# A two-layer masked attention stack in float32: from blocks of 256 tokens to two passes over blocks of 512 with seven-product projections

## The chip, the core and the metric

The kernel runs on one core of a Trainium2 chip. A core has a matrix engine (TensorE, PE in the rows; its weight loads are PEld), three engines for elementwise work (VectorE or DVE, ScalarE or ACT, GpSimd or POOL), a queue that issues transfers (SP), and on-chip memory in 128 partitions; matmul results land in PSUM, which has 8 banks. The engines run their own instruction streams in order and wait for each other by semaphores. The metric is the device time of one launch in microseconds (us). One profiled execution gives the rows that are read here.

## What is computed

The input is 128 batches of 64 tokens with 768 features, with one 64x64 adjacency matrix per batch. The tokens are normalised and clipped at zero; two layers follow, and the input is added to the result. Weights are 768x768 per layer and kind, all in float32.

```python
for l in range(L):
    m_left = jnp.einsum('bsh,oh->bso', h, W_left[l])
    m_right = jnp.einsum('bsh,oh->bso', h, W_right[l])
    u_left = jnp.einsum('bih,bjh->bij', h, m_left) / temper
    u_right = jnp.einsum('bih,bjh->bij', h, m_right) / temper
    u = u_left * adj_tri + u_left * diag_mask + u_right * jnp.swapaxes(adj_tri, 1, 2)
    delta_exp_u = jnp.exp(u) * adj
    attention = delta_exp_u / (jnp.sum(delta_exp_u, axis=2, keepdims=True) + 1e-10)
    h_lin = jnp.einsum('bsh,oh->bso', h, W_lin[l]) + b_lin[l]
    ctx = jnp.matmul(attention, h_lin)
    h = jax.nn.relu(_layer_norm(ctx, ln_a[l], ln_b[l]))
return h
```

## The kernel before

The 8192 tokens are cut into 32 blocks of 256. A unit is one block in one layer, so there are 64 units, and two neighbouring blocks alternate: both do layer 0, then both do layer 1. All six weight matrices stay on the chip. A unit runs through these parts:

- `projections` (L186): m_left and m_right, features on partitions. For each kind 6 output chunks of 6 matmuls over 256 tokens, 36 in all; two chunks share a PSUM bank, which ACT copies out (L188). Two banks take turns.
- `transposed` (L165): the *next* unit's normalised rows are turned so that features lie on partitions, 12 transposes; ACT clips them (L168 in layer 0, L171 in layer 1) into `ht`.
- `scores` (L199): 24 matmuls of 128 columns, then DVE masks (L204), ACT exponentiates (L208), DVE masks again.
- `linear` (L232): h_lin with tokens on partitions, 12 matmuls of 384 columns for each half of the block; DVE adds the bias while it empties the bank (L234). Between the halves stands `attention`: one matmul gives the row sums (L216), DVE takes the reciprocal (L221) and divides.
- `context` (L243): 4 matmuls of 384 columns; DVE takes mean and variance (L139, L140), ACT the root (L251), DVE normalises (L256). In layer 1 POOL then multiplies and adds two rows (L263, L264), DVE adds the input (L265), and POOL's queue stores the result (L267).

One matmul of the program is two instructions on PE in the trace, since the operands are float32; a transpose is one. Nothing schedules the work: every engine runs its instructions in the order in which the code emits them. `input_norm` of a coming block (L139, L149, L151, L153) is emitted at the start of a unit, ahead of that unit's projections, and behind the output work of the unit before. So ACT has the root L149 ahead of the copies L188 of the same unit, and L149 needs the statistics that DVE takes after L265, which needs POOL's L264.

## Time and profile before

| | us |
|---|---|
| median of 3 runs | 3959.29 (3958.76 to 3961.19) |
| span of the profiled execution | 3958.0 |
| PE busy | 3684.1 |
| DVE busy | 846.5 |
| ACT busy | 564.6 |
| POOL busy | 298.4 |

The profiled execution is one launch; its span runs from its first to its last instruction. Busy time is a union of instructions; PE's ends are modelled, so a price per matmul is better read from the distance of two starts than from a busy time. A number in square brackets at the end of a row is how long the engine sat idle before it, and what released it.

### The profile page before, as it was taken

The page shows a single profiled execution, that of the slowest core. Times are in us where ns is not written, and L with a number is a line of the kernel's source. Part 1 is how long each engine was busy: PE and PEld are TensorE (multiplying, and loading weights), DVE is VectorE, ACT ScalarE, POOL GpSimd, SP SyncE. Part 2 cuts the span into 40 slices and gives each one's busy share as a digit, 9 for nine tenths or more (in the row PEclk, how much of TensorE's full clock was granted, in tenths as well). Part 3 has the DMA queues.
Part 4 walks back from the last instruction along what each step waited for, and adds up shares of the span by engine and source line. Part 5 has one row for each costly group of instructions (what it writes and reads, how often), then busy time and mean ns, then how long its engine had stood idle before and what let it go on. Part 6 is the DMA issues. An engine that isn't in the chain of part 4 may idle for free.

```text
span 3958.0 us, 37169 instructions
## 1 busy us (share of the span) xinstructions
PE 3684.1 (93%) x16768; PEld 2914.2 (74%) x16768; DVE 846.5 (21%) x1826; ACT 564.6 (14%) x961; POOL 298.4 (8%) x270
## 2 busy tenths in 40 slices
PE   8989999899998999989999999999999999999997
PEld 6777777777776777777777777777777777777776
DVE  1122122221222222222222122121121211212212
ACT  1111111111111111111111111111111111111111
POOL 0010000100001000010000100000000000100001
PEclk9999999999999999999999999999999999999999
DMA  5010000100001000000000100000000000000000
GB/s 187 1 35 1 18 18 1 35 1 18 18 1 35 1 18 18 5 31 0 18 18 5 31 0 18 18 12 24 0 18 18 18 18 0 18 18 18 9 0 16
DMA packets 38942, 72.64 MB, mean 18 GB/s; under 512 B 3968, under 2 KB 25984, under 8 KB 38784
## 3 DMA queue, kind: packets, MB, share of 16 engines
q1 hardware_dynamic: 33664, 45.10, 3.9%
q0 software_dynamic: 5120, 25.17, 1.6%
q8 instruction: 131, 2.15, 0.2%
q14 instruction: 27, 0.22, 0.0%
HBM read 45.09 MB, written 25.17 MB: 18 GB/s over the span
## 4 chain that ended last, share of the span: by engine, by line
PE 83%; POOL 6%; DVE 4%; ACT 3%; issue 3%; SPq 1%; DMA 0%; POOLq 0%
PE mm L186 44%; PE mm L232 25%; PE aux L199 9%; PE cx L243 4%; POOL z L263 3%; POOL z L264 3%; DVE st L139 2%; ACT ht L171 1%; DVE z L265 1%; ACT mt L188 1%; PE aux L165 1%; POOL out_dram L267 0%; SPq L74 0%; ACT ht L168 0%; DVE mv L140 0%
## 5 line engine op out<-in xcount | busy, mean ns | idle before, releaser
L186 PE MATMUL mm<-ht,w_l 128*128 128x256 f32 x4608 | 1075.7, 396 | 202.4 <-ACT mt L188 202.4
L186 PEld LDWEIGHTS mm<-ht,w_l 128*128 128x128 f32 x4608 | 917.6, 200 | 363.4 <-ACT mt L188 214.9
L232 PE MATMUL mm<-w_n,ht 128*128 128x384 f32 x3072 | 1012.0, 486 | 0.0
L186 PE MATMUL mm<-ht,w_r 128*128 128x256 f32 x4608 | 1005.0, 379 | 0.0
L186 PEld LDWEIGHTS mm<-ht,w_r 128*128 128x128 f32 x4608 | 875.6, 190 | 118.9
L232 PEld LDWEIGHTS mm<-w_n,ht 128*128 128x128 f32 x3072 | 574.0, 190 | 373.0
L204 DVE TENSOR_TENSOR um<-aux,wm 64x256 f32<-64x256 f32 x128 | 54.0, 422 | 2053.0 <-PE aux L199 2052.2
L188 ACT COPY mt<-mm 128x512 f32<-128x512 f32 x384 | 221.0, 584 | 1517.3 <-PE mm L186 1517.3
L263 POOL TENSOR_TENSOR z<-z,a_row 128x768 f32<-128x768 f32 x64 | 116.1, 1813 | 3537.3 <-issue 3271.4
L199 PE MATMUL aux<-ht,mt 128*128 128x128 f32 x3072 | 359.8, 277 | 8.1 <-ACT ht L171 8.1
L199 PEld LDWEIGHTS aux<-ht,mt 128*128 128x128 f32 x3072 | 347.9, 192 | 18.0 <-ACT ht L171 15.7
L234 DVE TENSOR_TENSOR hl<-mm,blin 128x384 f32<-128x384 f32 x256 | 142.8, 558 | 662.8 <-PE mm L232 662.8
L243 PE MATMUL cx<-hl,att 128*128 128x384 f32 x512 | 175.6, 486 | 0.0
L251 ACT ACTIVATE sd<-var 128x2 f32<-128x2 f32 x64 | 13.0, 203 | 1084.7 <-DVE var L249 1084.7
L165 PE MATMUL aux<-ident,z 128*128 128x128 f32 x768 | 109.8, 280 | 42.7 <-ACT ht L171 23.1
L243 PEld LDWEIGHTS cx<-hl,att 128*128 128x128 f32 x512 | 97.3, 190 | 67.8
L139 DVE BATCH_NORM_STATS2 st<-cx 128x6 f32<-128x384 f32 x256 | 131.8, 557 | 48.0 <-PE cx L243 46.9
L165 PEld LDWEIGHTS aux<-ident,z 128*128 128x128 f32 x768 | 87.7, 142 | 64.5 <-ACT ht L171 30.7
L256 DVE TENSOR_SCALAR z<-cx,mv,rs 128x768 f32<-128x768 f32 x128 | 132.0, 1073 | 2.3
L264 POOL TENSOR_TENSOR z<-z,b_row 128x768 f32<-128x768 f32 x64 | 115.3, 1802 | 5.0
L265 DVE SCALAR_TENSOR_TENSOR z<-z,x 128x768 f32<-128x768 f32 x64 | 61.3, 958 | 240.2 <-POOL z L264 240.2
L171 ACT ACTIVATE ht<-aux,b_col,a_col 128x256 f32<-128x256 f32 x192 | 91.1, 577 | 0.0
(35 smaller groups left out, 700.5 us busy)
## 6 DMA issues: line engine op xcount, KB each, us to landing
x<-in_x_dram SPq DMA_DIRECT2D x32, 768.0 KB, 4.9
out_dram<-z POOLq DMA_DIRECT2D x64, 384.0 KB, 2.6
w_l<-in_w_left_dram SPq DMA_DIRECT2D x6, 768.0 KB, 7.6
w_r<-in_w_right_dram SPq DMA_DIRECT2D x6, 768.0 KB, 10.6
w_n<-in_w_lin_dram SPq DMA_DIRECT2D x6, 768.0 KB, 10.7
adj<-in_adj_dram SPq DMA_DIRECT2D x32, 128.0 KB, 5.7
blin<-in_b_lin_dram SPq DMA_DIRECT2D x2, 384.0 KB, 9.2
a_row<-in_ln_a_dram SPq DMA_DIRECT2D x1, 384.0 KB, 8.4
```

The lines of the kernel that those rows point to most:

```text
L139: nc.vector.bn_stats(st[:, n, :], src[:, n, :])
L165: nc.tensor.transpose(p[:, c, q * P:(q + 1) * P], z[:, q, (c0 + c) * P:(c0 + c + 1) * P], ident)
L171: nc.scalar.activation(ht[:, c0 + c, :], p[:, c, :], AF.Relu, bias=b_col[:, c0 + c:c0 + c + 1], scale=a_col[:, c0 + c:c0 + c + 1])
L186: nc.tensor.matmul(p[:, o, :], w[:, c, (o0 + o) * P:(o0 + o + 1) * P], ht[:, c, :], start=(c == 0), stop=(c == C - 1))
L188: nc.scalar.copy(mt[:, k, o0:o0 + 2, :], p)
L199: nc.tensor.matmul(p[:, q, k, :], mt[:, k, c, t], ht[:, c, t], start=(c == 0), stop=(c == C - 1))
L232: nc.tensor.matmul(p, ht[:, c, q * P:(q + 1) * P], W[l, "n"][:, c, cols], start=(c == 0), stop=(c == C - 1))
L234: nc.vector.tensor_add(hl[:, q, cols], p, blin[l][:, cols])
L243: nc.tensor.matmul(p[:, n, :HH], att[:, q, :], hl[:, q, n * HH:(n + 1) * HH], start=True, stop=True)
L256: nc.vector.tensor_scalar(z[:, q, :].rearrange("p (n d) -> p n d", n=2), ps[q][:, :, :HH], mv[:, q, 0:1], rs[:, q:q + 1], op0=ALU.subtract ...
L263: nc.gpsimd.tensor_mul(z[:, q, :], z[:, q, :], a_row)
L264: nc.gpsimd.tensor_add(z[:, q, :], z[:, q, :], b_row)
```

## The change

Each layer is now two passes over all tokens, in 16 blocks of 512. `pass_one` computes the projections, the scores and the attention, and stores the attention (and in layer 0 the clipped, turned input) in DRAM. `pass_two` loads the features and the attention again, computes h_lin, the context and the normalisation, and stores the next layer's features in DRAM, or the output. In the code of the order below, X, Y, Z and V are PSUM tiles of a bank each, `n` is a buffer that holds m, h_lin or the features to be stored, `ts` holds sums of token blocks.

The three projections are no longer multiplied out in full but by seven products of half matrices: the weight is cut into four blocks A11 to A22 of 384x384, the features of a block into B11 to B22 (384 features by 256 tokens each). Four sums of weight blocks (S1 to S4, on DVE or POOL, once per weight) and four sums of token blocks (T1 to T4, on POOL, once per block and pass) go into the seven products. For 512 tokens, m_left or m_right takes 63 matmuls of 256 columns where it took 72, and h_lin 42 of 384 columns where it took 48. Four PSUM banks hold the products, two of them accumulate a second product in the bank of a first that has been read in between, and DVE and ACT combine them. The elementwise work of neighbouring blocks is put in a queue of closures, and `pump` emits one (pass one) or three (pass two) of them behind each product. In pass two ACT applies the normalisation (L399), where DVE did (L256). The reciprocal, the bias and the output work stay on their engines; the output is stored through SP.

All of the old body goes. The core of what comes:

```diff
+    Q = 4
+    T = Q * P
+    TH = T // 2
...
+    big = ctx.enter_context(tc.tile_pool(name="big", bufs=2))
...
+    ps_st = ctx.enter_context(tc.tile_pool(name="ps_st", bufs=1, space=bass.MemoryType.PSUM))
+    ps_aux = ctx.enter_context(tc.tile_pool(name="ps_aux", bufs=4, space=bass.MemoryType.PSUM))
...
+    queue = deque()
+    def pump(n):
+        for _ in range(min(n, len(queue))):
+            queue.popleft()()
...
+    def load_w(l, kind):
+        v = SRC[kind][l].rearrange("(c p) o -> p c o", p=P)
+        t = {}
+        for s in ("A11", "A21", "A22", "A12", "S1", "S2", "S4"):
+            t[s] = wpool.tile([P, CH, HH], F32, name=f"w_{kind}_{s}")
+        for s in ("A11", "A21", "A22", "A12"):
+            i, o = int(s[2]) - 1, int(s[1]) - 1
+            nc.sync.dma_start(t[s], v[:, i * CH:(i + 1) * CH, o * HH:(o + 1) * HH])
+        W[l, kind] = t
+    def sums_w(l, kind, eng):
+        t = W[l, kind]
+        eng.tensor_add(t["S1"], t["A21"], t["A22"])
+        eng.tensor_sub(t["S2"], t["S1"], t["A11"])
+        eng.tensor_sub(t["A21"], t["A11"], t["A21"])
+        t["S3"] = t.pop("A21")
+        eng.tensor_sub(t["S4"], t["A12"], t["S2"])
+    ORDER = (("X", "A11", "B11"), ("Y", "S2", "T2"), ("Z", "S1", "T1"), ("V", "S3", "T3"),
+             ("X", "A12", "B21"), ("Z", "S4", "B22"), ("V", "A22", "T4"))
...
+        ts = big.tile([P, 4, CH, TH], F32, name="ts")
+        TS[key] = ts
+        b = tokens_of(key)
+        queue.append(lambda: nc.gpsimd.tensor_sub(b["T1"], b["B12"], b["B11"]))
+        queue.append(lambda: nc.gpsimd.tensor_sub(b["T2"], b["B22"], b["T1"]))
+        queue.append(lambda: nc.gpsimd.tensor_sub(b["T3"], b["B22"], b["B12"]))
+        queue.append(lambda: nc.gpsimd.tensor_sub(b["T4"], b["B21"], b["T2"]))
...
+                m = M[kind]
+                bank = {}
+                for i, (at, a, t) in enumerate(ORDER):
+                    new = at not in bank
+                    if new:
+                        bank[at] = ps_st.tile([P, 512], F32, name=at)
+                    p = bank[at][:, :TH]
+                    for c in range(CH):
+                        nc.tensor.matmul(p, w[a][:, c, g * P:(g + 1) * P], b[t][:, c, :],
+                                         start=(new and c == 0), stop=(c == CH - 1),
+                                         skip_group_check=True)
+                    if i == 0:
+                        s1 = sp.tile([P, TH], F32, name="s1")
+                        nc.scalar.copy(s1, p)
+                    elif i == 1:
+                        u2 = sp.tile([P, TH], F32, name="u2")
+                        nc.vector.tensor_add(u2, p, s1)
+                    elif i == 2:
+                        u4 = sp.tile([P, TH], F32, name="u4")
+                        nc.vector.tensor_add(u4, p, u2)
+                    elif i == 3:
+                        nc.vector.tensor_add(m[:, CH + g, TH:], p, u4)
+                    elif i == 4:
+                        nc.scalar.copy(m[:, g, :TH], p)
+                    elif i == 5:
+                        nc.vector.tensor_add(m[:, g, TH:], p, u2)
+                    else:
+                        nc.vector.tensor_add(m[:, CH + g, :TH], p, u2)
+                    pump(1)
...
+            for u in range(NB):
+                if u == 0:
+                    load(0)
+                    if first:
+                        first()
+                    prepare(0)
+                    flush()
+                    load(1)
+                for g in range(CH):
+                    project(u, "l", g)
+                    if g == 0:
+                        if u:
+                            scores(u - 1, 1, "r")
+                            if u + 1 < NB:
+                                load(u + 1)
+                        if u + 1 < NB:
+                            prepare(u + 1)
+                        if u in aside:
+                            aside[u]()
+                for g in range(CH):
+                    project(u, "r", g)
+                    if g == 0:
+                        scores(u, 0, "l")
+                flush()
+            scores(NB - 1, 1, "r")
+            flush()
+    def load_h(which, l, u):
+        ht = big.tile([P, C, T], F32, name="ht")
+        nc.sync.dma_start(ht, (H0 if l == 0 else H1)[u])
+        HT[which, l, u] = ht
...
+                z = sp.tile([P, H], F32, name="z", bufs=2 if last else 4)
+                Z[u, q] = z
+                if last:
+                    xr = sp.tile([P, H], F32, name="xr", bufs=2)
+                    nc.sync.dma_start(xr, x_t[u][q])
+                def chain():
+                    mv = stat.tile([P, 2], F32, name="mv1")
+                    mean_var(mv, cx)
+                    var = stat.tile([P, 1], F32, name="var")
+                    nc.vector.tensor_scalar(var, mv[:, 1:2], UNBIASED, 1e-30, op0=ALU.mult, op1=ALU.max)
+                    yield
+                    sd = stat.tile([P, 1], F32, name="sd1")
+                    nc.scalar.activation(sd, var, AF.Sqrt)
+                    rs = stat.tile([P, 1], F32, name="rs1")
+                    nc.vector.tensor_scalar_add(rs, sd, EPS_LN)
+                    nc.vector.reciprocal(rs, rs)
+                    nb = stat.tile([P, 1], F32, name="nb1")
+                    nc.vector.scalar_tensor_tensor(nb, mv[:, 0:1], -1.0, rs, op0=ALU.mult, op1=ALU.mult)
+                    yield
+                    for n in range(2):
+                        nc.scalar.activation(z[:, n * HH:(n + 1) * HH], cx[n], AF.Identity, bias=nb, scale=rs)
+                    yield
+                    if last:
+                        nc.gpsimd.tensor_mul(z, z, rows["a"])
+                        nc.gpsimd.tensor_add(z, z, rows["b"])
+                        yield
+                        nc.vector.scalar_tensor_tensor(xr, z, 0.0, xr, op0=ALU.max, op1=ALU.add)
+                        nc.sync.dma_start(out_t[u][q], xr)
+                it = chain()
+                return [lambda: next(it, None)] * (5 if last else 4)
...
+            def finish(u, r):
+                a = context(u, r)
+                pump(1)
+                b = context(u, 2 + r)
+                for i in range(len(a)):
+                    queue.append(a[i])
+                    queue.append(b[i])
+                if not last:
+                    turn(u, r)
+            def linear(u, r, before):
+                b, w = tokens_of((2, l, u)), W[l, "n"]
+                if r == 0:
+                    HL[u] = big.tile([P, Q, H], F32, name="n")
+                hl = HL[u]
+                bank = {}
+                for i, (at, a, t) in enumerate(ORDER):
+                    new = at not in bank
+                    if new:
+                        bank[at] = ps_st.tile([P, 512], F32, name=at)
+                    p = bank[at][:, :HH]
+                    for c in range(CH):
+                        nc.tensor.matmul(p, b[t][:, c, r * P:(r + 1) * P], w[a][:, c, :],
+                                         start=(new and c == 0), stop=(c == CH - 1),
+                                         skip_group_check=True)
+                    if i == 0:
+                        s1 = sp.tile([P, HH], F32, name="s1", bufs=1)
+                        nc.vector.tensor_add(s1, p, rows["b1"])
+                    elif i == 1:
+                        u2 = sp.tile([P, HH], F32, name="u2", bufs=1)
+                        nc.vector.tensor_add(u2, p, s1)
+                        u2b = sp.tile([P, HH], F32, name="u2b", bufs=1)
+                        nc.gpsimd.tensor_add(u2b, u2, rows["b2"])
+                    elif i == 2:
+                        u4 = sp.tile([P, HH], F32, name="u4", bufs=1)
+                        nc.vector.tensor_add(u4, p, u2b)
+                    elif i == 3:
+                        nc.vector.tensor_add(hl[:, 2 + r, HH:], p, u4)
+                    elif i == 4:
+                        nc.vector.tensor_add(hl[:, r, :HH], p, rows["b1"])
+                    elif i == 5:
+                        nc.vector.tensor_add(hl[:, 2 + r, :HH], p, u2)
+                    else:
+                        nc.vector.tensor_add(hl[:, r, HH:], p, u2b)
+                    if i == 0 and before:
+                        before()
+                    pump(3)
+            for u in range(NB):
+                if u == 0:
+                    load(0)
+                    prepare(0)
+                    flush()
+                for r in range(2):
+                    before = None
+                    if u or r:
+                        before = lambda: finish(*((u, 0) if r else (u - 1, 1)))
+                    linear(u, r, before)
+                    if r == 0:
+                        if u + 1 < NB:
+                            load(u + 1)
+                        if u in aside:
+                            aside[u]()
+                    elif u + 1 < NB:
+                        prepare(u + 1)
+                        flush()
+            finish(NB - 1, 1)
+            flush()
...
+    def weights(*pairs):
+        for l, kind in pairs:
+            load_w(l, kind)
+            queue.append(lambda l=l, kind=kind: sums_w(l, kind, nc.gpsimd))
+    def start():
+        load_w(0, "l")
+        sums_w(0, "l", nc.vector)
+        load_w(0, "r")
+        sums_w(0, "r", nc.vector)
+        load_w(0, "n")
+        sums_w(0, "n", nc.gpsimd)
+    pass_one(0, start, {})
+    pass_two(0, {1: lambda: weights((1, "l")), 2: lambda: weights((1, "r"))})
+    pass_one(1, None, {1: lambda: weights((1, "n"))})
+    pass_two(1, {})```

In PE's order, a unit before stands so (one row per group of matmuls: destination, operands, columns, count; this is the second unit, with the transposes of the third):

```order
L186 MATMUL mm<-ht,w_l_85 128x256 x36
L186 MATMUL mm<-ht,w_r_89 128x256 x36
L165 MATMUL aux<-ident,z 128x128 x12
L199 MATMUL aux<-ht,mt 128x128 x24
L232 MATMUL mm<-w_n_93,ht 128x384 x12
L216 MATMUL aux<-d,bsum 128x128
L232 MATMUL mm<-w_n_93,ht 128x384 x12
L243 MATMUL cx<-hl,att_138 128x384 x4
```

PE now, from the start, one third of the left projection's outputs for 512 tokens:

```order
L204 MATMUL aux<-ident,x 128x128 x24
L235 MATMUL X<-ht,w_l_A_175 128x256 x3
L235 MATMUL Y<-ts,w_l_S_180 128x256 x3
L235 MATMUL Z<-ts,w_l_S_179 128x256 x3
L235 MATMUL V<-ts,w_l_A_176 128x256 x3
L235 MATMUL X<-ht,w_l_A_178 128x256 x3
L235 MATMUL Z<-ht,w_l_S_181 128x256 x3
L235 MATMUL V<-ts,w_l_A_177 128x256 x3
```

Where a run of 36 matmuls stood, a bank now changes after every 3, and X, Z and V are each written twice within seven products.

DVE in an output unit before, from the context's variance on (layer 1, then the coming block's statistics):

```order
L249 TENSOR_SCALAR var<-mv_801 128x2
L253 TENSOR_SCALAR rs_820<-sd_818 128x2
L254 RECIPROCAL rs_820<-rs_820 128x2
L256 TENSOR_SCALAR z<-cx,mv_801,rs_820 128x768 x2
L265 SCALAR_TENSOR_TENSOR z<-z,x 128x768 x2
L139 BN_STATS st<-x 128x6 x2
```

DVE now, in the last pass, from the second product (Y) of one `linear` to its last (V):

```order
L463 TENSOR_TENSOR u_17097<-Y,s_17056 128x384
L393 TENSOR_SCALAR rs_17103<-sd_17101 128x1
L394 RECIPROCAL rs_17103<-rs_17103 128x1
L396 SCALAR_TENSOR_TENSOR nb_17106<-mv_17079,rs_17103 128x1
L468 TENSOR_TENSOR u_17116<-Z,u2b 128x384
L405 SCALAR_TENSOR_TENSOR xr<-z,xr 128x768
L470 TENSOR_TENSOR n<-V,u_17116 128x384
L405 SCALAR_TENSOR_TENSOR xr<-z,xr 128x768
L472 TENSOR_TENSOR n<-X,b_14084 128x384
L474 TENSOR_TENSOR n<-Z,u_17097 128x384
L476 TENSOR_TENSOR n<-V,u2b 128x384
```

The two instructions that wait for POOL's output work (L265 before, L405 now) stood together after a unit's last bank was emptied; now each stands between two instructions that empty banks of the products.

POOL now, in pass two of layer 0 around the loading of a layer-1 weight (before, there are no such sums, and POOL takes no part in a projection):

```order
L465 TENSOR_TENSOR u2b<-u_6170,b_5960 128x384
L96 TENSOR_TENSOR w_l_S_6238<-w_l_A_6235,w_l_A_6236 128x1152
L97 TENSOR_TENSOR w_l_S_6239<-w_l_S_6238,w_l_A_6234 128x1152
L98 TENSOR_TENSOR w_l_A_6235<-w_l_A_6234,w_l_A_6235 128x1152
L100 TENSOR_TENSOR w_l_S_6240<-w_l_A_6237,w_l_S_6239 128x1152
L465 TENSOR_TENSOR u2b<-u_6291,b_5960 128x384
```

The four sums of a weight stand ahead of the `u2b` (L465) of the same `linear`, for which DVE's L468 waits.

## Rows read from the trace of the kernel before

**Rows 1.** The page, busy time of each engine.

```profile
PE 3684.1 (93%) x16768; PEld 2914.2 (74%) x16768; DVE 846.5 (21%) x1826; ACT 564.6 (14%) x961; POOL 298.4 (8%) x270
```

**Rows 2.** The waits: engine, line, waited for, us in total, times, longest.

```profile
PE mm L186 <- ACT mt L188: 202.4, 31, 8.4
```

**Rows 3.** The timeline around one such wait: start, length, engine, line, tiles, count.

```profile
2175.05 0.96 DVE L265 SCALAR_TENSOR_TENSOR z<-z,x 128x768 f32<-128x768 f32 x1 [4.63 <-POOL z L264]
...
2178.34 0.29 ACT L149 ACTIVATE sd<-mv,eps_in 128x2 f32<-128x2 f32 x1 [14.25 <-DVE mv L140]
2178.54 1.05 ACT L188 COPY mt<-mm 128x512 f32<-128x512 f32 x2
...
2179.16 7.62 PE L186 MATMUL mm<-ht,w_l 128*128 128x256 f32 x24 [6.46 <-ACT mt L188]
2186.62 3.62 PE L186 MATMUL mm<-ht,w_r 128*128 128x256 f32 x16
```

**Rows 4.** Stretch behind that wait: PE, PEld, DVE, ACT, POOL busy, clock, DMA, GB/s.

```profile
2179.16:2186.40 7.24, 7.24 (x23) 6.01 (x24) 0.98 (x2) 0.43 (x1) 0.00 (x0) 0.69 0.34 126
```

**Rows 5.** The timeline of one undisturbed unit of layer 1, PE.

```profile
2047.18 15.70 PE L186 MATMUL mm<-ht,w_l 128*128 128x256 f32 x72
...
2062.72 15.70 PE L186 MATMUL mm<-ht,w_r 128*128 128x256 f32 x72
...
2078.26 1.04 PE L165 MATMUL aux<-ident,z 128*128 128x128 f32 x8
...
2080.02 0.66 PE L165 MATMUL aux<-ident,z 128*128 128x128 f32 x4 [0.72 <-ACT ht L171]
...
2080.93 5.62 PE L199 MATMUL aux<-ht,mt 128*128 128x128 f32 x48 [0.25 <-ACT ht L171]
...
2086.39 7.91 PE L232 MATMUL mm<-w_n,ht 128*128 128x384 f32 x24
...
2094.36 7.91 PE L232 MATMUL mm<-w_n,ht 128*128 128x384 f32 x24
...
2102.10 2.74 PE L243 MATMUL cx<-hl,att 128*128 128x384 f32 x8
...
2104.68 15.70 PE L186 MATMUL mm<-ht,w_l 128*128 128x256 f32 x72
```

**Rows 6.** Groups by form: line, engine, tiles, count, busy us, mean ns, idle before.

```profile
L234 DVE TENSOR_TENSOR hl<-mm,blin 128x384 f32<-128x384 f32 x256 | 142.8, 558 | 662.8 <-PE mm L232 662.8
L139 DVE BATCH_NORM_STATS2 st<-cx 128x6 f32<-128x384 f32 x256 | 131.8, 557 | 48.0 <-PE cx L243 46.9
L263 POOL TENSOR_TENSOR z<-z,a_row 128x768 f32<-128x768 f32 x64 | 116.1, 1813 | 3537.3 <-issue 3271.4 <-DVE z L256 265.3
L171 ACT ACTIVATE ht<-aux,b_col,a_col 128x256 f32<-128x256 f32 x192 | 91.1, 577 | 0.0
L208 ACT ACT_TABLE_LOAD x64 | 82.1, 1283 | 1.1
L265 DVE SCALAR_TENSOR_TENSOR z<-z,x 128x768 f32<-128x768 f32 x64 | 61.3, 958 | 240.2 <-POOL z L264 240.2
L221 DVE RECIPROCAL r<-s 128x128 f32<-128x128 f32 x64 | 61.0, 953 | 2.2
L204 DVE TENSOR_TENSOR um<-aux,wm 64x256 f32<-64x256 f32 x128 | 54.0, 422 | 2053.0 <-PE aux L199 2052.2
L153 DVE TENSOR_SCALAR z<-x,mv,rs 128x768 f32<-128x768 f32 x64 | 40.6, 677 | 1.2
```

**Rows 7.** The start: a stretch as in group 4, and PE's first uninterrupted run.

```profile
0.00:20.00 20.00, 9.77 (x37) 8.22 (x38) 4.05 (x11) 3.37 (x5) 2.74 (x16) 1.00 0.96 310
...
40.32 15.70 PE L186 MATMUL mm<-ht,w_r 128*128 128x256 f32 x72
```

**Rows 8.** The page: transfer, count, KB each, us from issue to landing.

```profile
x<-in_x_dram SPq DMA_DIRECT2D x32, 768.0 KB, 4.9
```

**Rows 9.** The timeline at the end: the last addition on DVE.

```profile
3950.08 0.96 DVE L265 SCALAR_TENSOR_TENSOR z<-z,x 128x768 f32<-128x768 f32 x1 [4.62 <-POOL z L264]
```

More of the change, by code (lines that the diff above doesn't have):

```diff
@@ L1 @@
 import math
+from collections import deque
 from contextlib import ExitStack
@@ L125 @@
     nc.vector.tensor_scalar(tri[:, 1, :], diff, 0.0, None, op0=ALU.is_lt)
[L127 to L137 removed]
+    BD = []
+    for i in range(2):
+        t = const.tile([P, Q, P], F32, name=f"bd{i}")
+        nc.gpsimd.memset(t, 0.0)
+        BD.append(t)
```

359 lines of the change are left out of this document (172 added, 187 removed).

## Prediction

> **What bounds the kernel now.** I read the busy times first: PE is busy for 93% of the span, and no engine of elementwise work for more than 21% [rows 1]. So the time is PE's work plus PE's waits. The waits give the second part: 31 times PE waits for ACT's copy of a projection bank, 202.4 us in all [rows 2]. The timeline shows why. DVE ends its output work late because it waits for POOL its first row in [rows 3], only then takes the coming block's statistics, ACT's root sits behind these and the two copies sit behind the root; PE has stood still for 6.46 us. It pays twice: in the stretch behind the wait the mean granted clock is 0.69 [rows 4], so part of it ran at 1.2 in the place of 2.4 GHz, and the 24 instructions took 7.46 us from start to start [rows 3]. In an undisturbed unit, 72 such instructions take 62.72 - 47.18 = 15.54 us [rows 5], so 24 take 5.18. The loss of clock is about 2.1 us (2.3 here; I take somewhat less as a mean), and a wait costs 8.6 us.
>
> The undisturbed unit gives the prices, from start to start [rows 5]. One matmul of the program is two instructions. At 256 columns it costs 15.54/36 = 0.432 us; at 384 columns (2102.10 - 2094.36)/12 = 0.645; a score of 128 columns (2086.39 - 2080.93)/24 = 0.2275. Four context matmuls take 2.58, as 384 columns should. Eight transposes are 1.04 us, 0.13 each, but twelve last from 2078.26 to 2080.93, 2.67 us, since the bank that they need waits for ACT: 1.11 us lost per unit of layer 1. The whole unit takes 57.5 us.
>
> **What goes.** All sums are against the profiled span of 3958.0 us; the median of the runs is 1.3 us above it.
> - Left and right projections: 64 units of 72 matmuls are 4608. Now 16 blocks x 2 layers x 2 kinds x 63 are 4032. 576 x 0.432 = 249 us less, all on PE, which sets the end.
> - h_lin: 1536 matmuls become 16 x 2 x 42 = 1344. 192 x 0.645 = 124 us less.
> - The wait for ACT: the input statistics now lie in pass one and the output work in pass two, so the chain of [rows 3] cannot form. One of the 31 waits belongs to the start, costed below. 30 x 8.6 = 258 us less.
> - The transposes' wait: the new transposes stand in groups of 4 or 8 between products, with four banks. 32 units x 1.11 = 36 us less.
>
> What stays as it is: 1536 scores, 256 context matmuls, 768 transposes, the row sums.
>
> **What the products cost beside PE's work.** In pass one a product takes 3 x 0.432 = 1.3 us. The bank written soonest again is X, two products after its last reader is emitted; the others have three or more. DVE's add of 256 columns lies between 0.42 (64 partitions, same length) and 0.56 us (384 columns) [rows 6]. So a bank has 2.6 us for less than 0.8 with the hand-over, and one more queued item fits between: statistics of a row tile are about 1.3, a normalised row tile 0.68 us [rows 6]. The reciprocal doubles in width, an estimate of 1.9 us from 953 ns, and stands in a slot whose bank ACT empties. POOL's four token sums are four instructions as wide as the 1813 ns one, 7.3 us against a block of over 65 us. I cost pass one at nothing beyond PE's own work; if that cover fails, it is the last rival.
>
> **Start.** PE's first run at full rate begins at 40.32 [rows 7], with 12 transposes and one projection done before, 1.6 + 15.5 us: 23 us lost. Now DVE has eight sums of weights (1152 elements, an estimate of 1.36 us each by the 768 elements in 958 ns) ahead of the first block's statistics, and four of them need the right weights. x, adjacency, left and right weights are 6.55 MB, at 310 GB/s [rows 7] 21 us, and 2 more until they can be used; the sums end at about 26.7. Statistics 4 x 1.3, the table load 1.28 [rows 6] and the root 0.3, four normalisations 2.7: 36.3. Transposes and ACT's clipping, 5.7: 42. T1 and T2 on POOL 3.6: PE's second product starts at 45.7, with 3.1 + 1.3 us done. Lost 41.3, and 2 for the clock: 43, 20 more than before.
>
> **Three changes of pass.** They are new; nothing is queued behind the last scores that PE could do. From the end of pass one: masks 2 x 0.42 [rows 6], and, as estimates by the same group at 256 elements, sum 0.43, exponential 0.4, mask 0.43, row sums 0.6, addition 0.4, reciprocal 1.9, product 0.4, with hand-overs 5.9 us. SP is in order: the attention's store waits for that, and behind it stand the bias and column loads (0.7 us or less each) and then the load of the features. That is 8.7. A 768 KB load lands in 4.9 us [rows 8]; twice the size at 310 GB/s adds 2.5: 16.5. T1 and T2 give 20.1. The row sums and the first product lie within; 17.7 remain, and 2.1 for the clock: 20 us. In layer 1 two full rows are loaded ahead: 22. From pass two to pass one: context, statistics, root, normalisation, transposes and clipping take 11.7 us, then a store and a load of 1.5 MB follow on one queue, and T1 and T2; with PE's share taken off between 18 and 22, so 20, and 2 for the clock. In all 64 us (ends: 40, if loads and sums overlap, and 90).
>
> **Layer-1 weights.** The left and right weights of layer 1 are loaded and summed in pass two, on POOL, ahead of the `u2b` of the running `linear`. Four sums of 1152 elements are 4 x 2.7 = 10.9 us, an estimate by the 1813 ns for 768 [rows 6]. SP issues these loads behind the store of layer-0 results and the load of the next block, 5.5 MB or 18 us. DVE waits for u2b with the other banks queued behind it, and PE stops at the sixth product, which writes Z. I take 10 us each and 2 for the clock, 24 (ends 0 and 28). The third weight is summed in pass one, where POOL is not waited for.
>
> **Pass two.** A `linear` is 7 x 1.935 us of products, with 2.58 of context behind the first. Count from its start. The second half of the context ends at 4.5; DVE's two statistics chains (two of 557 ns [rows 6] and two small ones, 1.5 in all) end at 6.4; roots, reciprocals and the second product's add interleave; ACT normalises from 7.1, two instructions per tile at 0.6, an estimate by the 577 ns of L171 [rows 6]: 8.3 and 9.5. In layer 0, four transposes need both tiles behind the third product, which ends at 8.4. PE waits 1.1 us, 32 times: 35. In layer 1, POOL multiplies and adds, four times 1.8 us [rows 6], after u2b at 8.6: 12.3 and 16.0. DVE's two final additions of 0.96 [rows 6] wait for these, and the adds that empty V and then X are emitted behind them. X is empty at 17.6, the next `linear` would start at 16.1. PE waits 1.5, 32 times: 49. POOL's token sums (8.6 us with the copies of the attention) follow at 16.0 and end before the next u2b. Ends for the two: 0, if ACT is twice as quick, and 180.
>
> **End.** From the last DVE addition's end at 3951.04 [rows 9] to the end of the span were 7 us; the chain keeps its length. 1 less.
>
> The sum: 3958 - 249 - 124 - 258 - 36 + 20 + 64 + 24 + 35 + 49 - 1 = 3482; with 1.3, **3484 us**.
>
> **Rivals.**
> - DVE and POOL exclude each other while both read on-chip memory. The final additions of DVE read two operands there, and each meets a POOL instruction of the other tile; before, the addition starts when POOL is done and has it to itself [rows 3]. Each `linear` of the last pass then ends 0.96 later: 32 x 0.96 = 31, so 3515. No row of before shows both at once, so nothing speaks against it. The Trainium skill, page "SBUF — State Buffer", section "SBUF: two separate sides", says that a VectorE instruction with two SBUF inputs and a GpSimd instruction that reads SBUF lock each other out for a whole instruction; by that rule this rival is the case.
> - Hand-overs of pass two cost more than 0.03 to 0.1 us. About ten stand in the chain of a `linear`; at 0.15 more each, 64 x 1.5 = 96: 3580. For it: the chain crosses engines more often than any of before, with adds that empty banks in between. Against: DVE and ACT follow each other closely in [rows 3] (0.2 us from the start of a root of 0.29 to the copy).
> - ACT is quicker than estimated and the weights come early, so that the two waits of pass two halve and the weights cost little: 3484 - 42 - 20 = 3422.
> - Groups of 3 do not run at the price of a run of 36: each of the 1792 products has its own wait at its head. At 0.1 us each, 3484 + 179 = 3663. The undisturbed unit has no such gap at the change of a bank after 12 matmuls.
> - The other side: the same gap from 0.265 us on, (3959 - 3484)/1792, makes the change slower, for instance 0.3: 4022. It needs banks that come free only after 2.9 us; I found 0.8.
>
> **How the numbers follow.** Chances: 0.45 for the forecast, 0.25 for the exclusion, 0.12 for long hand-overs, 0.08 for the quick case, 0.06 for the small gap; 0.03 for slower and 0.01 for the narrow place about no change (within 0.2%, about what a measurement of this kernel can tell from none). Faster is 0.96. The range goes from 3420, the quick case, to 3580, the long hand-overs; what it leaves out is the gap cases and the outer ends of start, pass changes and weights, some 2 in 10.
>
> **What would show it.** In the profile after: PE start to start of 1.3 us per product in pass one with no wait named between; no wait of a copy behind a root; three gaps of 15 to 22 us, each followed by a stretch of lower clock; two waits near 10 us in the first pass two; PE waiting in front of transposes (layer 0) and in front of X (layer 1), with DVE's L405 waiting for POOL. If a block of pass one takes over 71 us in layer 0 or 68 in layer 1 (products 54.4, scores 10.9, row sums 0.4, transposes 3.1 in layer 0), the cover of the banks fails and the forecast is wrong.

## The result, and the profile after

The changed kernel takes 3459.74 us (median; 3458.57 to 3461.1) beside 3960.24 us for the kernel before in the same session: a ratio of 0.8736, 95% interval 0.8724 to 0.8748. The forecast was 3484, with 3420 to 3580 as its range; the measured time is 24 us below the forecast. The profiled execution has a span of 3456.8 us (3958.0 before), and all sums below are against it.

The page's busy time of each engine:

```profile
PE 3258.6 (94%) x15168; PEld 2574.7 (74%) x15168; DVE 1347.1 (39%) x2938; ACT 537.1 (16%) x1137; POOL 887.6 (26%) x576
```

Beside [rows 1], PE is busy for 425.5 us less and for about the same share of the span: it still sets the time, with a tenth fewer instructions. DVE has 1.6 times the work (1347.1 beside 846.5 us) and POOL three times (887.6 beside 298.4), and most of that lies beside PE. What does not shows in PE's waits (engine, tile and line, what was waited for; us in total, times, longest):

```profile
PE aux L204 <- DVE x L198: 37.3, 2, 34.9
PE X L455 <- DVE n L472: 36.4, 30, 2.0
PE X L455 <- DMA ht<-h: 29.0, 2, 15.5
PE V L455 <- DVE n L470: 23.6, 31, 0.8
PE Z L455 <- DVE u L468: 19.0, 2, 9.5
PE aux L421 <- ACT z L399: 17.6, 31, 2.3
PE X L235 <- DMA ht<-h: 12.3, 1, 12.3
```

The row of [rows 2], ACT's copy with 202.4 us, is gone. In its place stand one start (L204), three changes of pass (two of X L455 and the one of X L235), two waits for the sums of layer 1's weights (Z L455), short waits in front of transposes in layer 0's second pass (L421), and two rows of short waits in the last pass (X for L472 and V for L470). The stretches of the program show where each lies (the columns are those of [rows 4]; the stretches are the first pass one, the change behind it, the first pass two, the second pass one and the last pass):

```profile
46.28:1133.00 1086.72, 1086.72 (x5952) 977.36 (x5952) 379.43 (x872) 172.71 (x340) 130.42 (x78) 1.00 0.14 51
1133.00:1153.57 20.57, 4.64 (x10) 2.14 (x8) 4.30 (x7) 1.70 (x2) 4.65 (x4) 0.59 0.53 192
1153.57:1752.60 599.03, 565.49 (x1966) 340.61 (x1966) 256.88 (x661) 180.49 (x372) 174.39 (x134) 0.98 0.23 88
...
1774.60:2821.70 1047.10, 1047.07 (x5592) 942.24 (x5592) 292.48 (x617) 77.17 (x207) 143.09 (x82) 1.00 0.08 29
...
2844.40:3441.00 596.60, 536.01 (x1594) 300.32 (x1594) 378.41 (x723) 89.01 (x186) 402.14 (x250) 0.99 0.33 122
```

Both passes one are clean: PE is busy for the whole stretch at a clock of 1.00. The two passes two lose 33.5 and 60.6 us of idle PE, the change shown has PE idle for 15.9 of 20.6 us and the rest at 0.59, and the other two (1752.60 to 1774.60 and 2821.70 to 2844.40) are alike.

Inside a pass one, the timeline of PE at the head of two neighbouring blocks (start, length, engine, line, tiles, count) shows one product every 1.29 to 1.30 us, with no wait named between them:

```profile
516.67 1.46 PE L235 MATMUL X<-ht,w_l_A 128*128 128x256 f32 x6
...
584.85 1.46 PE L235 MATMUL X<-ht,w_l_A 128*128 128x256 f32 x6
586.15 1.46 PE L235 MATMUL Y<-ts,w_l_S 128*128 128x256 f32 x6
```

Three matmuls of 256 columns by the price from [rows 5] are 3 x 0.432 = 1.30. The forecast's condition on the banks holds. From 516.67 to 584.85, a block of layer 0 takes 68.2 us.

The last pass is where DVE and POOL set PE's pace throughout. The timeline in a `linear` of r = 1 there, with PE, DVE and POOL:

```profile
2868.88 1.81 POOL L402 TENSOR_TENSOR z<-z,a 128x768 f32<-128x768 f32 x1
2868.95 2.54 DVE L405 SCALAR_TENSOR_TENSOR xr<-z,xr 128x768 f32<-128x768 f32 x1 [2.82 <-POOL z L403]
...
2870.76 2.40 POOL L403 TENSOR_TENSOR z<-z,b 128x768 f32<-128x768 f32 x1
2871.42 0.55 DVE L470 TENSOR_TENSOR n<-V,u 128x384 f32<-128x384 f32 x1
...
2872.02 2.20 PE L455 MATMUL V<-w_n_A,ts 128*128 128x384 f32 x6 [0.75 <-DVE n L470]
2873.12 1.80 POOL L120 TENSOR_TENSOR ts<-ht 128x768 f32<-128x768 f32 x1
2873.19 2.54 DVE L405 SCALAR_TENSOR_TENSOR xr<-z,xr 128x768 f32<-128x768 f32 x1 [1.23 <-POOL z L403]
...
2875.66 0.55 DVE L472 TENSOR_TENSOR n<-X,b 128x384 f32<-128x384 f32 x1
...
2876.26 3.58 PE L455 MATMUL X<-w_n_A,ht 128*128 128x384 f32 x6 [2.04 <-DVE n L472]
```

L405 is the addition that took 0.96 us in [rows 3]. Here it takes 2.54. The first one begins just behind POOL's L402 and ends 0.80 us after it (2868.88 + 1.81 = 2870.69, and 2871.49); POOL's L403 then takes 2.40, where it takes 1.80 alone, and ends at 2873.16. From 2868.88 on that makes 4.28 us for three instructions that alone take 1.81 + 0.96 + 1.80 = 4.57: they went one after the other but for 0.29 us. DVE came second, so its addition waited. The same holds for 47 of the 64 additions: in a `linear` of r = 1 both take 2.54 us, the second beside the token sums of the next block (L120); in one of r = 0 the first does, and the second, which finds POOL idle, takes 0.96. Behind L405 in DVE's queue wait the adds that empty V (L470) and X (L472), then PE. The X product behind the wait of 2.04 us takes 3.58 us here; behind most waits of this length it takes 2.20, as the last section shows.

### The profile page after: what moved, and what is told of

It reads as the page before. It is cut to its first block, busy times and chain, and to the rows that moved or that the text cites. A ratio compares the mean times of both kernels' runs of the same rounds, so it can differ in the third digit from the quotient of the medians.

```text
span 3456.8 us, 37506 instructions
## 1 busy us (share of the span) xinstructions
PE 3258.6 (94%) x15168; PEld 2574.7 (74%) x15168; DVE 1347.1 (39%) x2938; ACT 537.1 (16%) x1137; POOL 887.6 (26%) x576
## 4 chain that ended last, share of the span: by engine, by line
PE 82%; POOL 9%; DVE 5%; DMA 2%; ACT 1%; issue 1%; SPq 1%; POOLq 0%; ACTq 0%; DVEq 0%
PE V L235 14%; PE Z L235 14%; PE X L235 14%; PE aux L265 10%; PE Y L235 7%; PE X L455 6%; PE aux L374 5%; POOL z L403 4%; PE Y L455 4%; PE V L455 3%; POOL z L402 3%; PE Z L455 2%; DVE xr L405 2%; PE aux L204 1%; PE aux L421 1%; DVE u L463 1%
## 5 line engine op out<-in xcount | busy, mean ns | idle before, releaser
L120 POOL TENSOR_TENSOR ts<-ht 128x768 f32<-128x768 f32 x64 | 115.7, 1808 | 1592.8 <-DMA ht<-h 781.7
L265 PEld LDWEIGHTS aux<-ht,n 128*128 128x128 f32 x3072 | 352.0, 192 | 2.6
L265 PE MATMUL aux<-ht,n 128*128 128x128 f32 x3072 | 353.4, 275 | 0.0
L455 PE MATMUL X<-w_n_A,ht 128*128 128x384 f32 x768 | 280.5, 503 | 65.5 <-DVE n L472 36.4
L455 PE MATMUL V<-w_n_A,ts 128*128 128x384 f32 x768 | 271.6, 490 | 23.6 <-DVE n L470 23.6
L235 PE MATMUL X<-ht,w_l_A 128*128 128x256 f32 x1152 | 281.7, 381 | 12.3 <-DMA ht<-h 12.3
L235 PE MATMUL X<-ht,w_r_A 128*128 128x256 f32 x1152 | 280.1, 379 | 0.0
L235 PE MATMUL V<-ts,w_r_A 128*128 128x256 f32 x1152 | 280.0, 379 | 0.0
L235 PE MATMUL V<-ts,w_l_A 128*128 128x256 f32 x1152 | 280.0, 379 | 0.0
L455 PEld LDWEIGHTS X<-w_n_A,ht 128*128 128x128 f32 x768 | 144.3, 195 | 172.9 <-DVE n L472 54.9
L235 PEld LDWEIGHTS X<-ht,w_l_A 128*128 128x128 f32 x1152 | 217.4, 191 | 41.1 <-DMA ht<-h 12.7
L235 PEld LDWEIGHTS V<-ts,w_l_A 128*128 128x128 f32 x1152 | 218.8, 190 | 29.7
L235 PEld LDWEIGHTS V<-ts,w_r_A 128*128 128x128 f32 x1152 | 216.8, 190 | 28.3
L455 PEld LDWEIGHTS V<-w_n_A,ts 128*128 128x128 f32 x768 | 141.2, 190 | 128.0 <-issue 22.2
L235 PEld LDWEIGHTS X<-ht,w_r_A 128*128 128x128 f32 x1152 | 215.3, 190 | 27.3
L243 DVE TENSOR_TENSOR u<-Y,s 128x256 f32<-128x256 f32 x192 | 81.6, 425 | 360.6 <-PE Y L235 357.5
L465 POOL TENSOR_TENSOR u2b<-u,b 128x384 f32<-128x384 f32 x64 | 63.7, 995 | 551.3 <-DVE rs L393 551.2
L405 DVE SCALAR_TENSOR_TENSOR xr<-z,xr 128x768 f32<-128x768 f32 x64 | 135.8, 2123 | 130.9 <-POOL z L403 130.9
```

The costliest lines, as they stand in the source:

```text
L120: queue.append(lambda: nc.gpsimd.tensor_sub(b["T1"], b["B12"], b["B11"]))
L235: nc.tensor.matmul(p, w[a][:, c, g * P:(g + 1) * P], b[t][:, c, :], start=(new and c == 0), stop=(c == CH - 1), skip_group_check=True)
L243: nc.vector.tensor_add(u2, p, s1)
L265: nc.tensor.matmul(p[:, q, :], m[:, c, t], ht[:, c, t], start=(c == 0), stop=(c == C - 1))
L405: nc.vector.scalar_tensor_tensor(xr, z, 0.0, xr, op0=ALU.max, op1=ALU.add)
L455: nc.tensor.matmul(p, b[t][:, c, r * P:(r + 1) * P], w[a][:, c, :], start=(new and c == 0), stop=(c == CH - 1), skip_group_check=True)
```

## The experiments

### The waits alone

The kernel before, with `input_norm` of the coming block emitted between the left and the right projection:

```diff
-    def projections(b, l):
+    def projections(b, l, coming):
...
+            if k == 1 and coming is not None:
+                input_norm(coming)
...
-        if after and after[1] == 0:
-            input_norm(after[0])
-        mt = projections(b, l)
+        mt = projections(b, l, after[0] if after and after[1] == 0 else None)
```

> The kernel before, with one move: the statistics, root and normalisation of a coming block are emitted between the left and the right projection, where they stood ahead of both. Nothing else changes, nothing is left out. Theory (a wait of PE for ACT's copy costs its 6.46 us and 2.1 us of lost clock behind it): 30 waits x 8.6 = 258 us go, about 3700 us, and PE shows no wait for L188. Rival A (only the idle time counts, the lower clock is there for another reason): 194 us go, about 3765 us. Rival B (another wait takes its place, at the transposes, which now follow the normalisation more closely): above 3800 us.

Measured: 3687.44 us beside 3960.72, ratio 0.9311 (0.9297 to 0.9325). PE's longest row of waits there, in the transposes, is

```profile
PE aux L165 <- ACT ht L171: 23.2, 32, 0.7
```

The row of ACT's copy is gone, and 273.3 us with it: 31 waits at 8.8 us each, where 202.4 us stand in [rows 2]. The time is 13 us below the expected one and far from both rivals (3765, and above 3800). Of the other 71 us, 2.3 a time, most is the slower product behind each wait: in [rows 3] 7.46 us from start to start for what takes 5.18 at the full clock, and 7.10 behind the next wait, a loss of 2.3 and 1.9 in turn. So a reorder of the kernel before, without any change of the arithmetic, is worth more than half of what the whole change brought.

### The arithmetic alone

The changed kernel with eight full products in the place of seven, without the sums of weights and tokens; passes, blocks and queues as they are. A bank is emptied once, behind its second product, so that four instructions empty the banks of a group where seven did, and POOL's u2b goes too. The edit's core is the order of the products:

```diff
-    ORDER = (("X", "A11", "B11"), ("Y", "S2", "T2"), ("Z", "S1", "T1"), ("V", "S3", "T3"),
-             ("X", "A12", "B21"), ("Z", "S4", "B22"), ("V", "A22", "T4"))
+    ORDER = (("X", "A11", "B11"), ("X", "A12", "B21"), ("Y", "A11", "B12"), ("Y", "A12", "B22"),
+             ("Z", "A21", "B11"), ("Z", "A22", "B21"), ("V", "A21", "B12"), ("V", "A22", "B22"))
...
```

> The changed kernel with its two passes and blocks of 512, but with the projections multiplied out in full: eight products where seven stand, four PSUM banks, four instructions that empty them, no sums of weights or tokens on any engine. The result is the same function. Theory (the products are worth their matmuls and nothing else): 576 x 0.432 + 192 x 0.645 = 373 us of matmuls come back; the two waits of 9.5 us for sums of weights (22 with the clock), and the token sums ahead of each pass (3.6 us, three times, partly beside a product) go. 3460 + 373 - 22 - 5 = about 3805 us. So of the 500 us of the change, some 345 belong to the seven products and the rest to the order in two passes. Rival (products of 3 matmuls have a cost of their own at each change of bank): this kernel has fewer banks to empty, so clearly less than 3780.

Measured: 3684.03 us, ratio 0.9303 (0.9289 to 0.9317). This missed: seven products save 224 us in this kernel, not the 345 that stood in the expectation. PE's price per product is not the reason, since the products run at the same 1.295 us. The preparation that comes with seven products, and waits that this kernel doesn't show, are. The first products in PE's timeline, and then PE's waits, of this kernel:

```profile
18.35 2.76 PE L221 MATMUL X<-ht,w_l_A 128*128 128x256 f32 x12
```

```profile
PE X L430 <- DMA ht<-h: 28.8, 2, 15.4
...
PE X L221 <- DMA ht<-h: 12.0, 1, 12.0
...
PE aux L396 <- ACT z L374: 3.1, 2, 2.3
```

Without sums, the second product starts at 18.35 + 1.30 = 19.65, not at 46.28: 26.6 us. The rows of V and X in the last pass are empty, though the same addition (L380 here) still takes up to 2.545 us beside POOL; a bank's two products there take 3.87 us, and DVE is back in time. From the first linear product of the last pass to the end, this kernel takes 3683.1 - 3086.9 = 596.2 us, of which 32 x 1.94 = 62 are the eighth products; the changed kernel takes 3456.8 - 2840.4 = 616.4, so it loses 82 us that this one does not. The wait for weight sums (22 us with its slow product) and most of the wait in front of the transposes (14.5) are absent too. 26.6 + 82 + 22 + 14.5 = 145 of the 149 us by which 224 falls short of the 373 us that the forecast took for the products. Some 49 of these are the sums of weights and tokens in the open; the other 96 are waits of the passes two. Since the edit makes the products of a bank longer and also takes work from DVE and POOL, it doesn't show which of the two removes those waits. One thing more stands in these numbers: with full products, the two passes bring 276.7 us (3960.72 to 3684.03), hardly more than the 273.3 of the single move above.

### The last pass: order or exclusion

Two edits of the changed kernel, one for each cause. The first puts the final additions behind the last product, where no bank waits for DVE; DVE and POOL still meet. The second takes the addition's second operand from PSUM (`cx`, with a split by its two banks), so that it does not read two operands of on-chip memory; its place in the queue stays. It leaves out the addition of the input.

```diff
                 for i in range(len(a)):
+                    if i == 4:
+                        queue.extend([lambda: None] * 10)
                     queue.append(a[i])
                     queue.append(b[i])
```

> The changed kernel, with the two final additions of DVE (L405) in the last pass emitted behind the last product of a linear, where they stood behind the third and the fourth. Nothing is left out. Theory (the last pass loses 2.6 us per linear because X and V are emptied behind additions that wait for POOL): a linear falls from 18.7 to about 16.2 us, 32 x 2.5 = 80 us, about 3380 us; PE shows no wait for L470 or L472. Rival (POOL is the bound of the last pass, 25 us of work and waits in 35): PE then waits for u2b or the token sums in their place, and less than 30 us go.

```diff
-                        nc.vector.scalar_tensor_tensor(xr, z, 0.0, xr, op0=ALU.max, op1=ALU.add)
+                        for n in range(2):
+                            nc.vector.scalar_tensor_tensor(xr[:, n * HH:(n + 1) * HH], z[:, n * HH:(n + 1) * HH], 0.0,
+                                                           cx[n], op0=ALU.max, op1=ALU.add)
```

> The changed kernel, with the input's part of the final addition left out: the second operand of L405 is the context in PSUM in the place of the input in on-chip memory, in two halves of 384 columns. The output is therefore not the reference's. The two instructions together are a little longer than the one (2 x 0.56 against 0.96 us). Theory (a DVE instruction with two operands in on-chip memory and a POOL instruction exclude each other): no addition is stretched to 2.5 us and no POOL L403 to 2.4 us; a linear of the last pass falls from 18.7 to about 17.8, 25 to 30 us, about 3432 us. Rival (the hand-overs between the engines are slow): the additions still start late, and the time is that of the changed kernel or 5 us above it.

Measured: 3381.49 us for the first, ratio 0.8539 (0.8525 to 0.8553); 3414.68 for the second, ratio 0.8622 (0.8609 to 0.8635). The first met its expectation; V and X are no longer among PE's waits. The second gained 45 us, more than the 25 to 30 expected. Its timeline at the same place, and its row of waits for X (V has none):

```profile
2888.45 1.81 POOL L402 TENSOR_TENSOR z<-z,a 128x768 f32<-128x768 f32 x1
2888.52 1.02 DVE L406 SCALAR_TENSOR_TENSOR xr<-z,aux 128x384 f32<-128x384 f32 x2 [2.82 <-POOL z L403]
...
2890.34 1.80 POOL L403 TENSOR_TENSOR z<-z,b 128x768 f32<-128x768 f32 x1
...
2893.71 2.20 PE L457 MATMUL X<-w_n_A,ht 128*128 128x384 f32 x6 [0.93 <-DVE n L474]
...
PE X L457 <- DVE n L474: 27.3, 30, 0.9
```

The additions now run beside POOL's L402: 1.02 us for both halves, not 2.54, and POOL's L403 is 1.80 again. That settles the exclusion: the same engines meet at the same moments, and one operand lies elsewhere. The addition is also split in two, but the length of an instruction is not the reason: L470, 384 columns with one operand in PSUM, takes 0.55 us beside POOL's L403 in the rows of the changed kernel, and an instruction of one column with two operands in on-chip memory is held up (last section). PE's waits for X and V fall from 36.4 + 23.6 = 60.0 us to 27.3, 33 of the 45 us; three products at the lower clock (4.8 us in all, last section) are gone too, and the rest is the time that PE needs around each wait, about 0.2 us from start to start. What the order costs by itself is then what remains. The first and the last product into X of the last pass start as follows (count, shortest, middle and longest duration in ns, first and last start; the kernel after, the first edit, the second edit):

```profile
L455 PE MATMUL X<-w_n_A,ht x384: 486/486/1009, 2840.4 to 3432.6; 128*128 128x384 f32 x192
```

```profile
L457 PE MATMUL X<-w_n_A,ht x384: 485/486/1006, 2842.5 to 3353.7; 128*128 128x384 f32 x192
```

```profile
L457 PE MATMUL X<-w_n_A,ht x384: 486/486/1009, 2843.5 to 3390.2; 128*128 128x384 f32 x192
```

These are 592.2, 511.2 and 546.7 us, for 31 `linear`s and 12 us of a thirty-second: 18.7, 16.1 and 17.2 us each. PE's own work is 7 x 1.935 + 2.58 = 16.1. So order and exclusion together cost 2.6 us per `linear` in the mean, order without exclusion 1.1, and the exclusion in this order 1.5. Without the order, the exclusion costs PE nothing, though the additions of the first edit still take up to 2.56 us beside POOL.

### Sums of layer 1's weights, and the changes of pass

The first edit puts POOL's sums of the left and right weights behind the token sums of the coming block, no longer ahead of `u2b`. The second loads the features of the next pass's first block, and makes their token sums, during the last block of the pass before.

```diff
-            queue.append(lambda l=l, kind=kind: sums_w(l, kind, nc.gpsimd))
+            pending.append(lambda l=l, kind=kind: sums_w(l, kind, nc.gpsimd))
...
                     elif u + 1 < NB:
                         prepare(u + 1)
+                        queue.extend(pending)
+                        pending.clear()
                         flush()
...
```

> The changed kernel, with one thing moved: POOL's sums of the weights of layer 1 (4 x 2.61 us a kind, 1212.85 to 1223.25 in the trace) are put into POOL's queue behind the token sums and copies of the coming block, no longer ahead of u2b. Theory: TensorE's 9.5 us wait for u2b, twice, goes, and with it the 1.7 us at the lower clock behind each: 22 us less, about 3438 us, and no TensorE wait above 1 us on line 468. Rival: POOL's later work (token sums of the block, or the weights themselves where they are first needed) becomes late instead, and the time stays above 3452 us.

```diff
                             if u + 1 < NB:
                                 load(u + 1)
+                            else:
+                                load_h(2, l, 0)
                         if u + 1 < NB:
                             prepare(u + 1)
+                        else:
+                            sums_t((2, l, 0))
...
                         if u + 1 < NB:
                             load(u + 1)
+                        elif not last:
+                            load_h(1, 1, 0)
...
```

> The changed kernel, with one thing moved: at the three changes of pass the features of the next pass's first block are loaded, and their token sums made, during the last block of the pass before. Theory: the three gaps of 13.5, 12.3 and 15.5 us before the first product, with the row sums and the lower clock behind them (about 2 us each), were features and sums alone; 38 to 44 us less, about 3417 us, and no TensorE wait above 3 us on a DMA of ht. Rival: something else of the pass change is late right behind them (the rows of the biases, the last block's own tail), and less than 20 us is gained, the time staying above 3440 us.

Measured: 3443.0 us, ratio 0.8695 (0.8682 to 0.8708), and 3421.62 us, ratio 0.8642 (0.8628 to 0.8657). The late sums gain 17 us where 22 was expected: the wait of Z for u2b is gone from PE's waits, but the sums now meet other work. In that kernel, POOL and DVE in the next `linear`:

```profile
1226.18 2.62 POOL L101 TENSOR_TENSOR w_l_S<-w_l_A,w_l_S 128x1152 f32<-128x1152 f32 x1
...
1226.19 2.63 DVE L399 SCALAR_TENSOR_TENSOR nb<-mv,rs 128x1 f32<-128x1 f32 x1
```

One value per partition takes DVE 2.63 us, as long as POOL's sum beside it; ACT's normalisation waits for it, and PE's waits in front of the transposes grow from 17.6 us to

```profile
PE aux L424 <- ACT z L402: 22.0, 35, 2.3
```

The early features gain 38 us, the low end of what was expected. All waits for a DMA are gone, of 41.3 us; two more waits for u2b (5.2 us) stand behind them.

### All of them in one kernel

The late additions, the late sums, the early features, and the transposes of layer 0's second pass one product later:

```diff
                 if not last:
+                    queue.append(lambda: None)
                     turn(u, r)
```

> All in one kernel: the final additions behind the last product (78 us measured), the weight sums of layer 1 late (about 22), the features and token sums of the next pass early (about 40), and the transposes of layer 0's second pass one product later (16 of waits). If these stalls lie in different places, the gains add up: 3460 - 78 - 22 - 40 - 16 = 3304 us, taken as 3295 to 3320. Rival: they draw on the same slack of POOL and VectorE, and the sum falls short by a third or more, above 3355 us.

Measured: 3297.09 us, ratio 0.8325 (0.8313 to 0.8337). PE's waits in this kernel:

```profile
PE aux L205 <- DVE x L199: 38.2, 2, 35.9
PE Z L467 <- DVE u L480: 5.7, 2, 5.0
...
PE aux L430 <- ACT z L408: 3.1, 2, 2.3
```

The time lies in the expected range. The gains add up, and some more: 163 us, where 78 + 17 + 38 from the single edits leave 30. Of these, 19 are waits in front of transposes, which fall from 22.0 us to 3.1, DVE's stretched instruction beside the weight sums among them; 11 the rows don't assign. PE is busy for 98% of the span. Most of what is left of waits is the start.

## Why the prediction came out as it did

Point by point, in the order of the forecast's sum.

- **Products (-249 and -124).** As priced: 1.295 us for three matmuls of 256 columns, 1.94 for three of 384, start to start. That this is not the worth of the arithmetic in this kernel was not seen: eight products cost 224 us more, not 373, since the seven come with sums in the open and with waits in the passes two that the kernel with eight doesn't have. Part of this (start, weights, pass two) the forecast had in its other terms; it had not set it against the products.
- **ACT's copy (-258).** The mechanism was right. The experiment with the late statistics gives 8.8 us per wait, the forecast had 8.6: 30 waits are 264, 6 us more.
- **The transposes' wait (-36).** Gone as forecast: the transposes of the features for layer 1 now stand in layer 0's second pass, and what they wait for there is that term below.
- **Pass one at nothing beyond PE.** Right. A block of layer 0 took 68.2 us, the forecast's parts make 68.8; in layer 1 1047.1/16 = 65.4 for 65.7. The small differences lie in scores and transposes, 16 x 0.6 + 16 x 0.3 = 14 us less in all.
- **Start (+20).** Second product at 46.28, forecast 45.7. The parts were less exact than their sum: the four normalised row tiles took 6.96 us from 31.89 on, not 2.7, since POOL sums weights beside them (in the kernel without sums such a tile takes 0.67 to 0.68 us each time), while the statistics were done earlier than forecast.
- **Three changes (+64).** Measured: 29.0 + 12.3 us of waits for features, 4.8 for the row sums, 2.3 + 0.8 for transposes, 0.9 for the token sums, and about 2 for the clock behind each, 56 us. 8 less. (The forecast's own terms for the first load of features, 8.7 + 4.9 + 2.5, make 16.1 and not 16.5.) The clock's loss can be read from the first change: X of 1149.75 runs to the start of Y at 1153.57, 3.82 us for 1.94.

```profile
1149.75 3.89 PE L455 MATMUL X<-w_n_A,ht 128*128 128x384 f32 x6 [13.52 <-DMA ht<-h]
1153.57 2.20 PE L455 MATMUL Y<-w_n_S,ts 128*128 128x384 f32 x6
```

- **Layer-1 weights (+24).** Two waits of 9.5 us and about 2 for the clock behind each, 23 us, and the place was as forecast, the sixth product, behind u2b on POOL:

```profile
1220.68 2.61 POOL L100 TENSOR_TENSOR w_l_S<-w_l_A,w_l_S 128x1152 f32<-128x1152 f32 x1
1223.25 0.99 POOL L465 TENSOR_TENSOR u2b<-u,b 128x384 f32<-128x384 f32 x1
...
1224.88 3.88 PE L455 MATMUL Z<-w_n_S,ht 128*128 128x384 f32 x6 [9.50 <-DVE u L468]
```

- **Layer 0's second pass (+35).** Mis-sized. From the first to the thirty-second `linear` there are 1731.86 - 1149.75 = 582.1 us; without the weights' 22.6 and the slow first product's 1.9 they are 557.6, or 18.0 each. The forecast had 16.1 + 1.56 for transposes + 1.1 of wait = 18.8. The wait is about half of the forecast's 1.1:

```profile
1191.86 0.27 PE L421 MATMUL aux<-ident,z 128*128 128x128 f32 x1
1192.61 0.55 PE L421 MATMUL aux<-ident,z 128*128 128x128 f32 x3 [0.47 <-ACT z L399]
...
1194.93 1.04 PE L421 MATMUL aux<-ident,z 128*128 128x128 f32 x8
```

  and the transposes together are cheaper than 12 x 0.13 (the eight from 1194.93 hold PE until the next product starts at 1195.80, 0.11 us each). 32 x 0.8 = 25 us less.
- **Last pass (+49).** Mis-sized the other way: 2.6 us per `linear`, 83 us. The forecast named the order (L470 and L472 behind L405), and its addition of 0.96 us was the one that [rows 3] show alone. The exclusion, a rival with a chance of 0.25, was the case as well. The Trainium skill, page "SBUF — State Buffer", section "SBUF: two separate sides", has the rule; the 2.54 us beside POOL, and 1.02 with one operand in PSUM, agree with it. But its price was not the 0.96 of the forecast's rival, 31 us. The rival took the addition's own length; in fact the addition came second and waited for POOL's instruction, 1.58 us longer (2.54 - 0.96), three times in two `linear`s, ahead of the adds for V and X: 1.5 per `linear`, 47 us by the three spans above. The slower clock has a small part in it, 4.8 us. Order alone was 1.1 per `linear`, where the forecast had 1.5.

- **End (-1).** From the end of the last addition, 3453.47, to the end of the span are 3.3 us, where 7.0 were: 3 less than forecast.

```profile
3452.51 0.96 DVE L405 SCALAR_TENSOR_TENSOR xr<-z,xr 128x768 f32<-128x768 f32 x1 [1.69 <-POOL z L403]
```

So the sum, 3482, came out 25 us above the span, with terms that were wrong in both directions: -6 -14 +1 -8 -1 -25 +34 -3 = -22, and some 3 us that the rows don't assign. The mechanisms of the forecast were at work, but that the total is this close is in part luck: layer 0's second pass and the last pass were off by 25 and 34 us the opposite way. A forecast by the rival, 3515, would have been further off, though its mechanism was at work: the terms around it were too high. The rival of a gap at each product is refuted by passes one, and long hand-overs by 0.47 us of wait in front of the transposes. The point on the other side, a gap at every product, never came near: it needs banks that are free only after 2.9 us, and the passes one show no wait. In the last pass a bank was that late, V behind the addition of 2.54 us (PE's product into it from 2865.30 on, its add's end at 2871.97), and PE's wait there was 0.75.

## What to carry to other kernels

When a stage is to have fewer products, ask what they bring with them that PE will wait for: here seven products in the place of eight took 373 us from PE and gave 149 of it back as waits and preparation, and four changes of order alone then took 163 us out. Put work that frees a bank ahead of work that only ends a result, in every queue, and read a VectorE instruction's time from a place where GpSimd runs beside it. And first look for the wait that costs more than its length: moving one statistic in the kernel before was worth 273 us with no new arithmetic.

## What the runs showed of the hardware that was not expected

The exclusion holds for the smallest instruction too. With 128x1 results and two operands in on-chip memory, L396 takes 0.16 us alone and 0.87 beside u2b, and its counterpart in the kernel with the late sums took 2.63 beside a sum of weights of 2.62. It seems not to need two tiles of on-chip memory as operands: the normalisation at the start (L198) reads one tile and two columns, and four of them took 6.96 us beside sums of weights, 2.7 in the kernel without sums. Rows of the kernel after:

```profile
1189.56 0.16 DVE L396 SCALAR_TENSOR_TENSOR nb<-mv,rs 128x1 f32<-128x1 f32 x1
...
1190.83 0.99 POOL L465 TENSOR_TENSOR u2b<-u,b 128x384 f32<-128x384 f32 x1 [9.23 <-DVE rs L393]
1190.98 0.87 DVE L396 SCALAR_TENSOR_TENSOR nb<-mv,rs 128x1 f32<-128x1 f32 x1
```

And a wait of PE does not always bring the lower clock. Behind PE's waits of 0.4 to 0.8 us in the last pass, six instructions take 2.17 to 2.20 us. Behind the fifteen waits of 2.04 us they take 2.20 twelve times; only at 2876.26, 3026.91 and 3214.82 they take 3.58, 3.90 and 3.89, 4.8 us more in all. Stretches of the kernel after (columns as in [rows 4]) behind the wait of 9.50 us, behind the first of 2.04, and behind the next of 2.04, with the product of the last:

```profile
1224.88:1231.00 6.12, 6.12 (x14) 3.55 (x15) 1.85 (x4) 0.00 (x0) 6.04 (x4) 0.72 0.00 0
...
2876.26:2879.84 3.58, 3.58 (x7) 2.03 (x8) 0.88 (x2) 0.00 (x0) 3.58 (x3) 0.59 0.80 243
2915.19:2918.77 3.58, 3.58 (x11) 2.19 (x12) 2.05 (x5) 0.00 (x0) 3.58 (x3) 1.00 0.81 261
...
2915.19 2.20 PE L455 MATMUL X<-w_n_A,ht 128*128 128x384 f32 x6 [2.04 <-DVE n L472]
```

At 0.72 and 0.59 part of the stretch ran at 1.2 in the place of 2.4 GHz; at 1.00 none did. The wait of 9.50 us so costs about 11.3, and those of 2.04 cost between 2.0 and 3.7. What singles out the three slow ones, the rows don't show.
